# Re-ordering weight-sum stores, row gathers and the first pair of a conditional block kernel

## The chip, the cores and the metric

The kernel runs on one core of a Trainium2 chip. The metric is the device time of one execution in microseconds (us). All tensors are 32-bit floats. The names of the engines are PE (TensorE), DVE (VectorE), ACT (ScalarE), POOL (GpSimd) and SP (SyncE, which here only issues DMAs). ACT and POOL issue DMAs too.

## The reference

An input x of 32 sequences of 128 tokens with 512 features goes through two residual halves. Each half is modulated by a condition vector of the sequence. The first half changes only the tokens that the mask marks (the last few of each sequence, some 500 of 4096); the second changes all tokens.

```python
emb = silu(t) @ ada_w + ada_b
shift, scale, gate_msa = split(emb, 3, axis=1)
norm = _layernorm(x) * (1.0 + scale[:, None]) + shift[:, None]
norm = where(m, norm, 0.0)
fwd = gelu(norm @ ssm_w1 + ssm_b1) @ ssm_w2 + ssm_b2
bwd = flip(... the same with bwd_w1, bwd_b1, bwd_w2, bwd_b2 on flipped tokens ...)
x = x + gate_msa[:, None] * where(m, fwd + bwd, 0.0)
shift_mlp, scale_mlp, gate_mlp = split(silu(t) @ ffada_w + ffada_b, 3, axis=1)
ff_norm = _layernorm(x) * (1.0 + scale_mlp[:, None]) + shift_mlp[:, None]
h = gelu(ff_norm @ ff_w1 + ff_b1)          # 512 -> 1024
return x + gate_mlp[:, None] * (h @ ff_w2 + ff_b2)   # 1024 -> 512
```

## The kernel before

**First half, on slots.** The marked tokens are numbered, and 512 slots of 128-token tiles (slot tiles 0 to 3) take their rows of x by indirect DMA. Slots go in two groups of two tiles: `hidden` computes the first matmul and gelu (`ph_s`, `h_s`), `project` the second matmul (`po_s`), and `keep_slots` the end: bias (L208), gate (L210), adding the slot's x (L301), and a store of the tile to `x1_rows` in DRAM (L302). If there are more than 512 marked tokens a loop at the end of the program takes the rest.

**Second half, in pairs.** The 4096 tokens go in four pairs; a pair p is two sides of four sequences (2 x 512 tokens). For each sequence of a pair, `take_first_half` (L671 to L682) issues one indirect gather on POOL that puts the finished slot rows of `x1_rows` over the rows of x that are already in SBUF; slots past a bound are skipped. Then come the layer norm's statistics (`Statistics.one`, L707 and L708, and `root`, L712 on DVE and the power L713 on POOL), `normalised` (L719), and a turn of tokens into features. The turn is done by DVE's 32 x 32 transpose (L1149 or L1254) and 16 small DMAs (`turned`, L746); ACT then scales and shifts (`scaled`, L729). Side 1 of pair 0 is turned on PE instead (`transposed`, L735, with DVE's scaling L727).

**Matmuls with fewer multiplications.** Both matmuls of the second half are split in two levels of seven products for eight (in the manner of Strassen and Winograd). For this, sums of weight quarters and of token quarters are needed:

- Four weight sums of ff_w1 (`weight_sums(1)` to `(4)`, L584) are computed once, stored to `t_rows` in DRAM (`store_weight_sums`, L588 and L589, two DMAs a sum, 512 and 384 KB), and read back as `tw` (`load_weights`, L853) once a pair for each sum.
- Sum 1 lies in two x tiles (`spare`) that a later load of x (`load_side`, L331) fills; sum 2 in `t_2`; sum 3 in a group of x tiles; sum 4 in a tile with the tag "s12", which pair 0's token sums take over.
- `TokenBlocks.one(1)` to `one(4)` (L776) are token sums of the outer level: s1, s2, the first half of the second side, and s4. `token_sums` (L836 to L846) are those of the inner level.

The first product (ff_w1) is `FirstProduct`. Its seven outer products j are "streams", run in the order `STREAMS = (1, 2, 5, 6, 3, 7, 4)`. Each stream has seven inner phases P1 to P7, four matmuls of 256 columns each (L907). `window(new, old, fill)` runs one stretch of seven phases: P5 and P1 of the new stream, P3 and P7 of the old, P2 and P6 of the new, P4 of the old. After phase n (0 to 6) it issues what was put in `fill[n]`. `put(w, n, f, ...)` asks for `f` after phase n of the window in which `STREAMS[w]` is new. After a phase, results are combined: ACT copies (L921, L953, L965), DVE additions from PSUM (L932, L937, L942, L951), POOL additions between SBUF tiles (`with_p5` L958, `after` L987, `late_sum` L991), and gelu on ACT (L869). The second product (ff_w2, L1087) is `SecondProduct` with its own fourteen steps, P1U, P5U, P1V, P5V and so on; its first steps are interleaved with the last phases of stream 4.

**What sets the order.** The whole program from the first slot on is under a manual schedule: each engine runs its instructions in the order of the program text, and each queue (SP, ACT, POOL) issues its DMAs in that order. The tile framework only adds waits, for data and for buffers that are used again. So an instruction that waits holds all later ones of its engine.

**The places that the change touches.** Pair 0 begins at L1132: five gathers on POOL, statistics of side 0, the root, three more gathers, `gate_rows`, and the store of sum 4 on POOL (L1141). Then come the second slot group's `hidden`, the turn of side 0 on both DMA queues, and the slot tiles 2 and 3 (L1167 to L1183) with side 1's turns between the matmuls of `project`. L1174 stores sums 1 and 2 on SP, L1175 loads half of pair 1's x. L1187 to L1211 are streams 1 and 2 of pair 0, written out by hand. The fills of the windows are put at L1220 to L1272; the gathers and statistics of the next pair are at L1260 to L1272.

Of the kernel before, what the change touches and what calls it, by code (L numbers as in the profile page):

```python
# [9 lines left out]
F32 = mybir.dt.float32  # L10
# [4 lines left out]
ALU = mybir.AluOpType  # L15
# [7 lines left out]
def kernel(  # L23
# [49 lines left out]
    nc = tc.nc  # L73
# [108 lines left out]
    def hidden(xT, n, w, bcol, func, name, pool, parts=range(HC)):  # L182

        h = []
        for f in parts:
            ph = ps_h.tile([P, 512], F32, tag="h", name=f"ph_{name}_{f}")
            for k in range(KC):
                nc.tensor.matmul(  # L188
                    ph[:, :n], w[:, k, ts(f, P)], xT[:, k, :], start=(k == 0), stop=(k == KC - 1)
                )  # L190
            t = pool.tile([P, n], F32, tag="h", name=f"h_{name}_{f}", bufs=HC + 2)
            nc.scalar.activation(t, ph[:, :n], func, bias=biasT[:, bcol + f : bcol + f + 1])  # L192
            h.append(t)
        return h
# [10 lines left out]
    def gated(po, bias, gate, name, between=lambda: None):  # L205

        t = tp.tile([P, D], F32, tag="t", name=f"t_{name}")
        nc.vector.tensor_tensor(t, po, bias, ALU.add)  # L208
        between()
        nc.vector.tensor_tensor(t, t, gate, ALU.mult)  # L210
        return t
# [84 lines left out]
    def finish_slots(at, h1, gate, between=None):  # L296
        keep_slots(at, project(at % (NC // 2), h1, w2, f"s{at}", between), gate)

    def keep_slots(at, po, gate, between=lambda: None):
        t = gated(po, b2, gate, f"s_{at}", between)  # L300
        nc.vector.tensor_tensor(t, t, xc[at], ALU.add)  # L301
        nc.sync.dma_start(x1_rows[ts(at, P), :], t)  # L302
# [98 lines left out]
    slot_row = ssm.tile([P, NS], F32, name="slot_row")  # L401
# [160 lines left out]
    def in_blocks(t):  # L562
        return t.rearrange("p g (h f) -> p (g h) f", f=2 * P)
# [22 lines left out]
    def store_weight_sums(*which, queue=nc.sync):  # L586
        for j in which:
            queue.dma_start(t_rows[j - 1, :, :4], t_sum[j][0])  # L588
            queue.dma_start(t_rows[j - 1, :, 4:], t_sum[j][1][:, :3])  # L589
# [76 lines left out]
    t = in_blocks(sp.tile([P, G, D], F32, tag="s12", name="tw_4"))  # L666
    t_sum[4] = [t[:, :4], t[:, 4:]]
# [464 lines left out]
    take_first_half(0, x_of[0], range(G + 1))  # L1132
    stats = [Statistics(x_of[0][side], f"0_{side}") for side in range(2)]
# [7 lines left out]
    store_weight_sums(4, queue=nc.gpsimd)  # L1141
# [24 lines left out]

    po_s2 = project(0, h1, w2, "s2")  # L1167
# [22 lines left out]
    now.apart(1)  # L1190
    now.do(1, "P1")
# [3 lines left out]
    of_x[0].one(4)  # L1195
# [16 lines left out]
    for p in range(NP):  # L1212
# [25 lines left out]
        if more_pairs:  # L1238
# [33 lines left out]
            put(6, 4, stats[1].root)  # L1272
# [189 lines left out]
```

## Time and profile before

| | us |
|---|---|
| median of 3 runs | 465.46 |
| lowest and highest | 465.28, 465.61 |
| the profiled execution | 467.79 |
| its span, first to last instruction | 466.0 |

The mean granted clock of TensorE is 0.995. Busy times in the span:

| engine | busy us | share |
|---|---|---|
| PE, matmuls | 451.4 | 97% |
| PE, weight loads | 365.3 | 78% |
| DVE | 330.8 | 71% |
| ACT | 175.4 | 38% |
| POOL | 160.0 | 34% |

DMA moved 70.41 MB. The stages on PE's timeline: slots of the first group to 53 us, the second group 59.1 to 88.4, then four pairs. The first product of pair 0 begins at 88.42, its second product at 135.6; later pairs take about 91.5 us each from one second product to the next (the step P5V starts at 148.87, 240.16 and 331.83).

A matmul of 256 columns has a duration of 379 ns in the list of groups, but matmuls overlap: a run of them starts one every 216 ns. So a busy share of 97% isn't the distance to PE's peak; the spacing of the starts is what to read.

In lines of the timeline the columns are start, duration, engine, line, operation, output<-inputs and shape, number of instructions merged, and in brackets the idle time before, with what ended it.

### The profile page before, as it was taken

How to read it: one execution, taken by the hardware profiler on the slowest of the kernel's cores; microseconds unless marked ns; L12 is line 12 of the kernel's file. 1: busy time of each engine (PE TensorE's matmuls, PEld its weight loads, DVE VectorE, ACT ScalarE, POOL GpSimd, SP SyncE). 2: the span in 40 equal slices, each digit the busy share in tenths (PEclk: the TensorE clock that was granted, in tenths of full speed). 3: DMA queues.
4: the chain of work that ended last, by engine and by line, in shares of the span. 5: the costliest groups of instructions: out<-in, count | busy, mean ns of one | idle time of the engine just before them, and what ended most of it. 6: DMA issues, size and time to landing. Idle time of an engine off the chain costs nothing.

```text
span 466.0 us, 5828 instructions
## 1 busy us (share of the span) xinstructions
PE 451.4 (97%) x2000; PEld 365.3 (78%) x2000; DVE 330.8 (71%) x538; ACT 175.4 (38%) x380; POOL 160.0 (34%) x153
## 2 busy tenths in 40 slices
PE   6899999899999999999999999999999999999995
PEld 2385385477788888888888888888888888888884
DVE  4649768969668759996787399867864995434645
ACT  3121021734364371354553713444546144562000
POOL 6210074038973000389710004897000025660000
PEclk9999999989999999999999999999999999999999
DMA  8999716880406752834086438330973342212022
GB/s 277 386 407 355 302 50 140 265 316 22 165 0 198 102 108 86 291 118 162 1 209 101 98 107 313 98 136 3 235 100 73 127 168 79 80 68 114 0 79 105
DMA packets 82418, 70.41 MB, mean 151 GB/s; under 512 B 63168, under 2 KB 63696, under 8 KB 81362
## 3 DMA queue, kind: packets, MB, share of 16 engines
q1 hardware_dynamic: 67298, 57.03, 40.0%
q0 software_dynamic: 4480, 11.66, 7.4%
q10 hardware_dynamic: 10608, 1.32, 2.0%
q8 instruction: 17, 0.28, 0.3%
q14 instruction: 15, 0.12, 0.1%
HBM read 56.83 MB, written 13.17 MB: 150 GB/s over the span
## 4 chain that ended last, share of the span: by engine, by line
PE 74%; POOL 8%; ACT 5%; issue 5%; DVE 4%; DMA 3%; SPq 0%; POOLq 0%; DVEq 0%
PE a_o L1087 19%; PE e_o L1087 16%; PE a_m L907 14%; PE e_m L907 11%; PE ph_s L188 6%; PE po_s L202 4%; POOL hb L991 2%; ACT hb L869 2%; POOL x L675 2%; DMA x<-in_x_dram 2%; DMA tw<-t_rows 1%; POOL ha L958 1%; DVE xT L727 1%; ACT ha L869 1%; PE part_s L283 1%
## 5 line engine op out<-in xcount | busy, mean ns | idle before, releaser
L958 POOL TENSOR_TENSOR ha<-p_m,ha 128x512 f32<-128x512 f32 x20 | 27.4, 1369 | 152.5 <-ACT ha L965 143.3
L1087 PE MATMUL e_o<-fw,ha 128*128 128x256 f32 x256 | 57.9, 379 | 0.0
L729 ACT ACTIVATE xT<-xT,modT 128x128 f32<-128x128 f32 x112 | 44.2, 480 | 29.4 <-DMA xT<-xn 29.4
L1087 PE MATMUL a_o<-t,hb 128*128 128x256 f32 x240 | 54.1, 379 | 0.0
L1087 PEld LDWEIGHTS e_o<-fw,ha 128*128 128x128 f32 x256 | 48.6, 190 | 6.6
L1087 PEld LDWEIGHTS a_o<-t,hb 128*128 128x128 f32 x240 | 45.6, 190 | 6.2
L675 POOL DMA_INDIRECT x<-x_rows,slot_i x32 | 37.5, 1173 | 26.9 <-DMA x_rows<-t_s 18.6
L869 ACT ACTIVATE hb<-hb,biasT 128x256 f32<-128x256 f32 x64 | 29.0, 501 | 28.1 <-POOL hb L991 19.4
L958 POOL TENSOR_TENSOR hb<-p_m,hb 128x512 f32<-128x512 f32 x20 | 28.3, 1415 | 23.0 <-DVE e_m L951 22.7
L921 ACT COPY p_m<-e_m 128x512 f32<-128x512 f32 x27 | 15.8, 586 | 50.1 <-PE e_m L907 50.1
L1087 PE MATMUL e_o<-fw,s 128*128 128x256 f32 x128 | 29.2, 381 | 0.5 <-DVE s L1041 0.3
L965 ACT COPY ha<-e_m 128x512 f32<-128x512 f32 x32 | 18.5, 579 | 28.5 <-PE e_m L907 26.9
L1087 PE MATMUL a_o<-fw,ha 128*128 128x256 f32 x128 | 28.9, 379 | 0.0
L1087 PE MATMUL a_o<-t,s 128*128 128x256 f32 x128 | 28.9, 379 | 0.0
L202 PE MATMUL po_s<-w,h_s 128*128 128x512 f32 x64 | 28.6, 592 | 0.0
L188 PE MATMUL ph_s<-xT_s,w 128*128 128x256 f32 x128 | 28.6, 382 | 0.0
L1087 PEld LDWEIGHTS e_o<-fw,s 128*128 128x128 f32 x128 | 24.1, 190 | 4.8 <-DVE s L1041 1.7
L188 PEld LDWEIGHTS ph_s<-xT_s,w 128*128 128x128 f32 x128 | 24.0, 190 | 4.7 <-ACT h_s L192 1.5
L1087 PEld LDWEIGHTS a_o<-t,s 128*128 128x128 f32 x128 | 24.3, 190 | 3.3
L1087 PEld LDWEIGHTS a_o<-fw,ha 128*128 128x128 f32 x128 | 24.3, 190 | 3.3
L932 DVE TENSOR_TENSOR e_m<-a_m,ha 128x512 f32<-128x512 f32 x20 | 13.9, 696 | 17.6 <-POOL ha L958 7.4
L869 ACT ACTIVATE ha<-e_m,biasT 128x256 f32<-128x256 f32 x48 | 20.1, 469 | 15.8 <-PE e_m L907 8.9
(207 smaller groups left out, 872.3 us busy)
## 6 DMA issues: line engine op xcount, KB each, us to landing
tw<-t_rows SPq DMA_DIRECT2D x16, 896.0 KB, 5.1
x<-in_x_dram SPq DMA_DIRECT2D x16, 512.0 KB, 6.8
gate<-gate_rows POOLq DMA_DIRECT2D x8, 1024.0 KB, 5.3
out_dram<-x SPq DMA_DIRECT2D x15, 512.0 KB, 3.3
xT<-xn SPq DMA_DIRECT2D x92, 64.0 KB, 2.8
fw<-in_L_cond_ff_w_dram SPq DMA_DIRECT2D x2, 2048.0 KB, 10.4
ada_f<-in_L_cond_ffada_w_dram SPq DMA_DIRECT2D x4, 768.0 KB, 15.4
ada_a<-in_L_cond_ada_w_dram SPq DMA_DIRECT2D x4, 512.0 KB, 7.0
```

The costliest lines, as they stand in the source:

```text
L188: nc.tensor.matmul(ph[:, :n], w[:, k, ts(f, P)], xT[:, k, :], start=(k == 0), stop=(k == KC - 1))
L202: nc.tensor.matmul(po, h[f][:, ts(i, P)], w[:, f, :], start=(f == 0), stop=(f == HC - 1))
L675: nc.gpsimd.indirect_dma_start(out=xs[i // G][i % G // 2][:, i % 2], out_offset=None, in_=x1_rows[:slots, :], in_offset=bass.IndirectOffse ...
L729: nc.scalar.activation(out, src, AF.Identity, bias=shift, scale=scale)
L869: nc.scalar.activation(dst[:, n], src[:, n], AF.Gelu_apprx_tanh, bias=biasT[:, f : f + 1])
L907: nc.tensor.matmul(bank[:, ts(n, QT)], self.w_block(j, product)[:, ts(n, P)], self.x_block(j, product), start=(product in ("P1", "P5") and ...
L921: nc.scalar.copy(p5, e)
L932: nc.vector.tensor_tensor(e, a, p5, add)
L958: nc.gpsimd.tensor_tensor(self.place(RESULT[j], c), self.p5[j], other, ALU.add)
L965: nc.scalar.copy(self.place(RESULT[j], c), src)
L991: nc.gpsimd.tensor_tensor(part, self.place("21", c), part, ALU.add)
L1087: nc.tensor.matmul(part, src[:, k, ts(i, P)], w[product][:, k, :], start=(last and k == 0), stop=True, skip_group_check=True,)
```

## The change

The change moves work and leaves the arithmetic as it is.

- Sum 1 is stored from POOL's queue right after pair 0's first five gathers; before, it was stored from SP after slot tile 3's `project`.
- Sum 4 is stored from SP after that `project`, ahead of sum 2; before, from POOL after the gathers. Each store now sends its second part (384 KB) first. Sum 4 lies in a tile with the tag "s4" and a tile that shares its place with `slot_row`, no longer in "s12". The `h` tiles have 8 buffers instead of 10.
- The end of slot tile 2 is split: bias, then side 1's turn 2, then gate, adding x and the store. The end of slot tile 3 is split too: bias, then one(2) and one(3), gate, and after P2, P5 and P6 of stream 1 the adding of x and the store. one(4) moves from after P6 to ahead of all of pair 0's products.
- Gathers for the next pair: four at the end of the window of stream 5 in pair 0 and of stream 2 in pairs 1 and 2, then one in the window of stream 6, one in that of stream 3, two in that of stream 7. Before, pair 0 had all eight in one place, and pairs 1 and 2 had four, two, one and one. With windows and phases: (2, 6) or (1, 6) four, (3, 4) one, (4, 6) one, (5, 4) two.
- Statistics: side 0's root goes to (5, 4) for all pairs (before (3, 6) for pairs 1 and 2). Side 1's four go to (4, 4), (5, 3), (6, 4), (6, 6) instead of (4, 4), (4, 6), (5, 3), (6, 4), and its root to (6, 6) instead of (6, 4).

```diff
-            t = pool.tile([P, n], F32, tag="h", name=f"h_{name}_{f}", bufs=HC + 2)
+            t = pool.tile([P, n], F32, tag="h", name=f"h_{name}_{f}", bufs=HC)
...
-    slot_row = ssm.tile([P, NS], F32, name="slot_row")
+    slot_row = ssm.tile([P, 6 * P], F32, tag="row", name="slot_row")[:, :NS]
...
     def store_weight_sums(*which, queue=nc.sync):
         for j in which:
+            queue.dma_start(t_rows[j - 1, :, 4:], t_sum[j][1][:, :3])
             queue.dma_start(t_rows[j - 1, :, :4], t_sum[j][0])
-            queue.dma_start(t_rows[j - 1, :, 4:], t_sum[j][1][:, :3])
...
-    t = in_blocks(sp.tile([P, G, D], F32, tag="s12", name="tw_4"))
-    t_sum[4] = [t[:, :4], t[:, 4:]]
+    t_sum[4] = [
+        in_blocks(sp.tile([P, KC // 2, G * S], F32, tag="s4", name="tw_4")),
+        ssm.tile([P, 6 * P], F32, tag="row", name="tw_4_b").rearrange("p (b f) -> p b f", b=3),
+    ]
     weight_sums(4)
...
     take_first_half(0, x_of[0], range(G + 1))
+    store_weight_sums(1, queue=nc.gpsimd)
...
     nc.gpsimd.dma_start(gate_rows, mod2[2 * B : 3 * B, :])
-    store_weight_sums(4, queue=nc.gpsimd)
...
+    def with_bias(at, po):
+        tail[at] = tp.tile([P, D], F32, tag="t", name=f"t_s_{at}")
+        nc.vector.tensor_tensor(tail[at], po, b2, ALU.add)
+
+    def with_gate(at, gate):
+        nc.vector.tensor_tensor(tail[at], tail[at], gate, ALU.mult)
+
+    def with_x(at):
+        nc.vector.tensor_tensor(tail[at], tail[at], xc[at], ALU.add)
+        nc.sync.dma_start(x1_rows[ts(at, P), :], tail[at])
+
     po_s2 = project(0, h1, w2, "s2")
 
     def keep_and_turn():
-        keep_slots(2, po_s2, gs[0])
+        with_bias(2, po_s2)
         turn(2)()
+        with_gate(2, gs[0])
+        with_x(2)
 
     po = project(1, h1, w2, "s3", {0: turn(0), 1: turn(1), 2: keep_and_turn, 4: turn(3)})
-    store_weight_sums(1, 2)
+    store_weight_sums(4, 2)
     x_of[1] = [load_side(1, 0, spare)]
     of_x[0] = TokenBlocks(0, xT)
     of_x[0].one(1)
-
-    def outer_sums():
-        of_x[0].one(2)
-        of_x[0].one(3)
-
-    keep_slots(3, po, gs[1], outer_sums)
+    with_bias(3, po)
+    of_x[0].one(2)
+    of_x[0].one(3)
+    with_gate(3, gs[1])
...
     now.apart(1)
+    of_x[0].one(4)
     now.do(1, "P1")
     now.seed(1)
     now.do(2, "P1")
     now.do(1, "P2", "P5", "P6")
-    of_x[0].one(4)
+    with_x(3)
     now.token_sums(1, 0)
...
-            if p == 0:
-                put(2, 6, take_first_half, 1, x_next, range(2 * G))
-            else:
-                put(1, 6, take_first_half, p + 1, x_next, range(G))
-                put(2, 6, take_first_half, p + 1, x_next, range(G, G + 2))
-                put(3, 4, take_first_half, p + 1, x_next, range(G + 2, G + 3))
-                put(5, 4, take_first_half, p + 1, x_next, range(G + 3, 2 * G))
+            put(2 if p == 0 else 1, 6, take_first_half, p + 1, x_next, range(G))
+            put(3, 4, take_first_half, p + 1, x_next, range(G, G + 1))
+            put(4, 6, take_first_half, p + 1, x_next, range(G + 1, G + 2))
+            put(5, 4, take_first_half, p + 1, x_next, range(G + 2, 2 * G))
             for i, at in enumerate(((3, 1), (3, 3), (3, 4), (3, 6))):
                 put(*at, stats[0].one, i)
-            put(*((3, 6) if p else (5, 4)), stats[0].root)
-            for i, at in enumerate(((4, 4), (4, 6), (5, 3), (6, 4))):
+            put(5, 4, stats[0].root)
+            for i, at in enumerate(((4, 4), (5, 3), (6, 4), (6, 6))):
                 put(*at, stats[1].one, i)
-            put(6, 4, stats[1].root)
+            put(6, 6, stats[1].root)
```

More of the change, by code (lines that the diff above doesn't have):

```diff
@@ L203, in project, with gated @@
         return po
-    def gated(po, bias, gate, name, between=lambda: None):
+    def gated(po, bias, gate, name):
         t = tp.tile([P, D], F32, tag="t", name=f"t_{name}")
         nc.vector.tensor_tensor(t, po, bias, ALU.add)
-        between()
         nc.vector.tensor_tensor(t, t, gate, ALU.mult)
@@ L294, in keep_gate, with finish_slots @@
         return t
[L296 to L300, printed above, removed]
+    def finish_slots(at, h1, gate):
+        t = gated(project(at % (NC // 2), h1, w2, f"s{at}"), b2, gate, f"s_{at}")
         nc.vector.tensor_tensor(t, t, xc[at], ALU.add)
@@ L1165, in turn @@
         return lambda: transposed(1, xn_b, xT[1], k)
+    tail = {}
+    def with_bias(at, po):
[6 more added lines that the diff above has]
+        nc.sync.dma_start(x1_rows[ts(at, P), :], tail[at])
     po_s2 = project(0, h1, w2, "s2")
     def keep_and_turn():
-        keep_slots(2, po_s2, gs[0])
+        with_bias(2, po_s2)
         turn(2)()
+        with_gate(2, gs[0])
+        with_x(2)
     po = project(1, h1, w2, "s3", {0: turn(0), 1: turn(1), 2: keep_and_turn, 4: turn(3)})
-    store_weight_sums(1, 2)
+    store_weight_sums(4, 2)
     x_of[1] = [load_side(1, 0, spare)]
```

## The prediction

> **What bounds the kernel now.** I read the page first: TensorE (PE) is busy 97% of the span, and the chain that ended last is 74% PE. So a change pays only where PE's starts come late. I looked for these in the timeline of PE: four matmuls of 256 columns start 0.864 us after the four before them where nothing holds them (102.57, 103.43, 104.29). What the starts take beyond that I call late time. From the first product matmul (88.42) to the second stream's P2 (100.73) eight groups take 12.31 us instead of 6.91: 5.4 us late. The next 31 groups of pair 0 (to 129.57) take 28.84 instead of 26.78: 2.06 late. The same 31 groups of pair 1 (193.90 to 220.85) are only 0.17 late. Later PE is late in one place a pair, 0.3 us before step P5V (148.87, 240.16, 331.83). So some 7.4 us can be won, all of it in the first pair.
>
> The waits of PE, longest first (us in total, times, longest):
>
> ```profile
> PE e_m L907 <- ACT e_m L953: 1.5, 1, 1.5
> PE e_m L907 <- DVE e_m L951: 1.1, 2, 0.7
> ...
> PE a_m L907 <- DVE t_s L208: 0.3, 1, 0.3
> ```
>
> The first is ScalarE's (ACT's) copy L953. The timeline shows why it comes late: ACT issues transposing DMAs until 83.84, waits for their landing, and scales 16 blocks before the copy.
>
> ```profile
> 83.84 1.28 ACT L1152 ACT_TABLE_LOAD   x1 [10.24 <-DMA xT<-xn]
> ...
> 85.60 6.26 ACT L729 ACTIVATE xT<-xT,modT 128x128 f32<-128x128 f32 x16 [0.27 <-DMA xT<-xn]
> ...
> 91.77 0.57 ACT L953 COPY e_m<-a_m_alone 128x512 f32<-128x512 f32 x1
> ...
> 92.40 1.59 PE L907 MATMUL e_m<-xT,fw 128*128 128x256 f32 x4 [1.52 <-ACT e_m L953]
> ```
>
> In the table of stretches (busy times, then clock, DMA share, GB/s) the DMA engines are full at 76 us, with the fourth weight sum among the small packets, and PE's clock is halved at 94 us, just after PE stood:
>
> ```profile
> 76.00:78.00 2.00, 2.00 (x6) 0.88 (x5) 0.78 (x3) 0.00 (x0) 1.04 (x1) 1.00 0.99 237
> ...
> 94.00:96.00 2.00, 2.00 (x6) 1.56 (x6) 0.00 (x0) 0.86 (x2) 0.00 (x0) 0.50 0.91 322
> ```
>
> In pair 0 eight gathers stand in a row on GpSimd (POOL), 104.24 to 116.3, and its sums L958 and L987 come after them; VectorE's (DVE's) L951 and PE wait for them, 0.6 us late at 120.83. Its last gather and the sum behind it:
>
> ```profile
> 115.31 0.99 POOL L675 DMA_INDIRECT x<-x_rows,slot_i  x1 [0.30 <-issue]
> 116.32 1.28 POOL L958 TENSOR_TENSOR ha<-p_m,ha 128x512 f32<-128x512 f32 x1
> ```
>
> The end of pair 1's first product, the place where the change may cost. DVE has no gap from 228.38 to 238.27, and its last link L942 releases an ACT gelu, then L1041, then PE:
>
> ```profile
> 228.38 0.70 DVE L932 TENSOR_TENSOR e_m<-a_m,ha 128x512 f32<-128x512 f32 x1 [1.35 <-POOL ha L958]
> ...
> 229.65 1.75 POOL L958 TENSOR_TENSOR hb<-p_m,hb 128x512 f32<-128x512 f32 x1
> ...
> 230.18 1.50 DVE L719 TENSOR_SCALAR xn<-x,mv,rstd 128x512 f32<-128x512 f32 x1
> ...
> 231.36 1.23 POOL L713 TENSOR_TENSOR rstd<-ve,half 128x4 f32<-128x4 f32 x1
> ...
> 233.54 0.65 DVE L937 TENSOR_TENSOR hb<-a_m,hb 128x512 f32<-128x512 f32 x1
> ...
> 237.59 0.68 DVE L942 TENSOR_TENSOR hb<-a_m,hb 128x512 f32<-128x512 f32 x1
> ...
> 239.42 1.29 DVE L1041 TENSOR_TENSOR s<-hb 128x512 f32<-128x512 f32 x2 [1.15 <-ACT hb L869]
> 240.16 3.32 PEld L1087 LDWEIGHTS e_o<-fw,s 128*128 128x128 f32 x16 [0.56 <-DVE s L1041]
> ```
>
> **What the Trainium skill says.** "SBUF — State Buffer", section Who interferes with whom: a GpSimd operation and a VectorE operation with two SBUF inputs, or a tensor_scalar in its two-port mode, shut each other out for a whole instruction. The trace agrees: L719 takes 0.51 alone and 1.50 beside L958; L712 takes 0.17 alone and 0.30 (226.72, 135.44, 318.39) ending just when a POOL sum ends. "TensorE: Matmul & The Clock Gate", What's actually happening: a free-running window of 3413 ns with too little work halves the clock. The trace has one such stretch of about that length, 92.9 to 96.3. "DMA: Bandwidth & Descriptors", Queues, rings and completion order: each DMA engine takes a queue's descriptors in ring order. The loads tw, issued at 93.85 and 94.3, landed in that order after 6.7 and 8.6 us.
>
> **The change part by part.**
>
> *Store of sum 1 on POOL between gathers 5 and 6.* Two issues of 0.60 and 0.54 us (the rows of the fourth sum's store at 73.07). POOL stood 1.57 us there before L713 (67.30), and DMA is 0.07 busy from 66 to 70. Gathers 6 to 8 land up to 1 us later; their statistics run from 74.17, 2.7 us after the landing of the sixth. Cost 0; if the cover were gone, 1.1.
>
> *Sum 4 leaves POOL.* 0.9 MB leave the stretch where the 16 transposing DMAs move 1.05 MB at about 130 GB/s. At the 385 GB/s of 86 to 90 us it had taken 2.4 us of the engines. So ACT's table load, scaling and copy come 2.4 us earlier: scaling 83.2 to 89.45, the copy right behind PE's first four matmuls (89.5), and P2 starts without a wait. Half of that, 1.2 us, would still leave one(4) below as the later one.
>
> *First pair reordered.* DVE does the same operations. with_bias(2), turn(2), gate and x take 2.7 us as before; the store of slots 2 is issued near 86.35 instead of 85.24, and on SP sums 4 and 2, half a side of x, and the two tw loads stand behind it. one(4) (1.22) moves ahead of L932, to 92.4 to 93.6; the store of sum 4 has landed by 91.4 (issue 87.2, landing 3.6 to 4.2), so it isn't waited for. P6 of stream 1 ends at 93.3 on an unheld PE, so L932 runs 93.6 to 94.25 instead of 97.05. From there with_x (0.6) stands where one(4) stood: L937 95.5, L951 96.1 to 96.8, PE at 96.85 instead of 100.73. Late time 1.5 instead of 5.4, 3.9 won; PE's idle window is gone and with it the half clock, whose 1.7 us are in the 5.4. Then the bill: stream 5 could start at 99.55, and its tw, landed at 100.5 before, has the queue start 1.1 us later and 0.26 MB less ahead (some 0.8 us): about 100.5. 0.9 lost (0 to 2). with_x(3)'s store is now behind the tw loads and lands near 103 instead of 98, so the four gathers run about 103.2 to 109.3; the sums L958 of stream 6 are wanted by 111.6, so this costs nothing.
>
> *Gathers spread.* Pair 0 has four in a row instead of eight. Its 2.06 late falls to about 0.5: 1.5 won. In pairs 1 and 2 there is nothing to win.
>
> *Gathers and statistics late in streams 5 and 6.* The sixth gather is issued near 217.1 in pair 1's times (POOL's sums before it, 1.25 each, end at 216.95) and lands 2.9 later at 220.0; its statistics stand at 219.05 in DVE's order. Then L712 meets the sum L991 (220.75 to 222.0), and L932, before at 220.64, ends near 222.85; PE wants it at 222.58. 0.3 late (0 to 0.9) in each of three pairs. The last two gathers and the root on POOL (1.05 each with gaps) end at 225.7, L991 was free at 225.62: 0.1.
>
> *Last statistics and root to the end of stream 7* (the position 6, 6). On POOL the root no longer stands ahead of L991 (232.57): 1.2 us earlier, but PE waited for DVE there, not for it. On DVE L707, L708 and L712 (0.6 + 0.2 + 0.2, from 225.78) leave a stretch with a gap (1.35 before 228.38) and enter the gapless one, behind L1041 (230.4). L712 arrives at 231.25, is held by L958 to 231.6; L991, which waits already, goes next to 232.95; L719 is held until then. L937 comes at 235.3 instead of 233.54, P4 of stream 4 on PE 0.4 late, L942 at 239.35 instead of 237.59, the gelu 240.05 to 240.95, L1041, PE at 241.7 instead of 240.16: 1.55 a pair. Without the two holds it is 0.6; with gathers of 1.4 instead of 1.05 it is 2.1. Behind L942 stand ACT's gelu and DVE's L1041, and PE has nothing else: it is all lost.
>
> *Buffers* (h two fewer, slot_row and half of sum 4 in one place, sum 4 no longer in s12): no instruction is added, and all earlier readers have ended by 57 us. 0.
>
> **Sum.** Won 3.9 - 0.9 + 1.5 = 4.5. Lost 3 x (1.55 + 0.3 + 0.05) = 5.7. Net +1.2 us. The profiled execution took 467.79 with a span of 466.0, 2.3 above the median of the runs, 465.46. The parts are differences, so they go onto the median: 466.7.
>
> **Rivals.**
> - *The ends of the pairs are cheap* (faster). The place is the DVE row L719 at 230.18: if it gets the port ahead of L991, or L712 isn't held, and the sixth gather lands before 219.5, a pair loses 0.7, not 1.9. Then -4.5 + 2.1 = -2.4: 463.1. For it: L719 (230.18) did get in ahead of L713, which took 1.23 instead of 1.05. Against: L991 would be waiting first. It decides below 1.5 us a pair.
> - *The first pair gives little.* The tw load or the store behind it lands 2 us later still, as SP's queue is full from 86 to 104 us (0.9 to 1.0 busy). Won 2: +3.7, 469.2. Against: fewer bytes are ahead of tw.
> - *The clock falls at P5V.* A gap of 1.5 to 2 us there halves it for a window of 3.4 us, 1.7 lost, in each of three pairs: 466.7 + 5.1 = 471.8. For it: one window with PE about half busy did that at 92.9. Against: this gap is shorter.
>
> **How the numbers follow.** Forecast 0.45, with its own range 465.8 to 468.2; cheap ends 0.27; little won 0.18; clock 0.10. A measurement of this kernel tells 0.2% (0.93 us) from no change. Faster: most of the second, 0.23. Same: the lower third of the forecast (0.15) and the upper edge of the second (0.04), 0.19. Slower 0.58. The range leaves out the clock case and the edges of the second and third: 462.6 to 470.2.
>
> **What would show it.** Right: the copy L953 near 89.5 and no half clock near 94; stream 5 starting 2.5 to 3.5 us earlier; no eight gathers in a row; L719 held behind L991 and PE about 1.5 us later before each of three P5V. Wrong: P5V no more than 0.7 late (then faster), or the transposing DMAs ending at the old time, which would leave L953 as the last wait.

## The result, and the profile after

The changed kernel took 467.57 us (median of 15 runs), the kernel before 465.75 beside it (15 runs): a ratio of 1.0032, 95% interval 1.0018 to 1.0047. It is slower by 1.8 us, where 1.2 were forecast.

The two profiles say something else. The profiled execution of the changed kernel took 466.66 (span 464.8), that of before 467.79 (span 466.0): by them the change won 1.1 us. So the profile of before lies 2.0 us above its median, and the profile after 0.9 below its own. The table splits the spans at four of PE's starts; the last column is a second profile of the changed kernel, from the experiments (467.07, also 0.7 below the median of its runs).

| stretch, us | before | changed | changed, second |
|---|---|---|---|
| to the first product of pair 0 | 88.42 | 88.00 | 87.52 |
| on to stream 5's first product | 15.01 | 12.44 | 11.88 |
| on to P5V of pair 0 | 45.44 | 45.13 | 46.90 |
| on to P5V of pair 1 | 91.29 | 92.77 | 92.68 |
| on to P5V of pair 2 | 91.67 | 92.58 | 92.55 |
| on to the end | 134.17 | 133.88 | 133.87 |
| span | 466.0 | 464.8 | 465.4 |

The first pair wins, later pairs lose 0.9 to 1.5 each. Which waits stand behind this is in the list of PE's waits of the changed kernel (us in total, times, longest). Lines of the helpers are 2 lower here, so that L1085 was L1087, L1039 was L1041, L951 was L953:

```profile
PE e_o L1085 <- DVE s L1039: 3.5, 3, 1.2
...
PE e_m L905 <- DMA tw<-t_rows: 1.1, 1, 1.1
...
PE e_m L905 <- DVE e_m L930: 0.5, 2, 0.2
```

ACT's copy, 1.5 us and first in the list of before, is gone. In its place P5V leads, three times 1.2. The timeline of the changed kernel shows the first pair:

```profile
81.50 1.28 ACT L1150 ACT_TABLE_LOAD   x1 [8.33 <-DMA xT<-xn]
...
83.26 6.26 ACT L727 ACTIVATE xT<-xT,modT 128x128 f32<-128x128 f32 x16 [0.27 <-DMA xT<-xn]
...
89.43 0.57 ACT L951 COPY e_m<-a_m_alone 128x512 f32<-128x512 f32 x1
...
90.10 1.09 PE L905 MATMUL e_m<-xT,fw 128*128 128x256 f32 x4
...
100.44 1.10 PE L905 MATMUL e_m<-sx,tw 128*128 128x256 f32 x4 [1.09 <-DMA tw<-t_rows]
```

The transposing DMAs released ACT 2.34 us earlier (81.50 instead of 83.84), the scaling starts at 83.26 instead of 85.60, and the copy at 89.43 no longer holds PE: P2 follows at 90.10 with no wait in brackets. At 100.44 PE stands 1.09 for the weight sum tw. In the table of stretches PE's clock, the figure before the DMA share, is whole where it was 0.50 in the profile of before:

```profile
94.00:96.00 2.00, 1.97 (x8) 1.41 (x8) 1.97 (x4) 0.40 (x1) 0.00 (x0) 1.00 0.82 256
```

The end of pair 1's first product in the changed kernel:

```profile
225.51 0.70 DVE L930 TENSOR_TENSOR e_m<-a_m,ha 128x512 f32<-128x512 f32 x1 [1.69 <-POOL ha L956]
...
226.79 1.74 POOL L956 TENSOR_TENSOR hb<-p_m,hb 128x512 f32<-128x512 f32 x1
...
227.32 0.69 DVE L705 BATCH_NORM_STATS2 st<-x 128x6 f32<-128x512 f32 x1
...
228.04 0.18 DVE L706 BATCH_NORM_AGGREGATE mv<-st 128x2 f32<-128x6 f32 x1
...
228.25 0.31 DVE L710 TENSOR_SCALAR ve<-mv 128x4 f32<-128x4 f32 x1
...
228.47 1.57 DVE L717 TENSOR_SCALAR xn<-x,mv,rstd 128x512 f32<-128x512 f32 x1
228.50 1.26 POOL L989 TENSOR_TENSOR hb<-hb 128x512 f32<-128x512 f32 x1
...
235.94 0.68 DVE L940 TENSOR_TENSOR hb<-a_m,hb 128x512 f32<-128x512 f32 x1
...
237.59 1.29 DVE L1039 TENSOR_TENSOR s<-hb 128x512 f32<-128x512 f32 x2 [0.97 <-ACT hb L867]
```

DVE has no gap from 225.51 to 236.62. From L930 to L940 it takes 10.43 us; the same stretch of before (L932 at 228.38 to L942 at 237.59) took 9.21. L710 ends within 0.03 us of POOL's L956 (228.56 and 228.53), and L717, which takes 0.50 to 0.53 in its next three places, takes 1.57 beside POOL's L989 (228.50 to 229.76).

### The profile page after: what moved, and what is told of

It is laid out like the page before. It is cut to its first block, busy times and chain, and to the rows that moved or that the text cites. A ratio compares the mean times of both kernels' runs of the same rounds, so it can differ in the third digit from the quotient of the medians.

```text
span 464.8 us, 5830 instructions
## 1 busy us (share of the span) xinstructions
PE 447.9 (96%) x2000; PEld 364.2 (78%) x2000; DVE 333.4 (72%) x538; ACT 176.2 (38%) x380; POOL 158.5 (34%) x153
## 3 DMA queue, kind: packets, MB, share of 16 engines
q10 hardware_dynamic: 10608, 1.32, 2.0%
## 4 chain that ended last, share of the span: by engine, by line
PE 57%; DVE 9%; POOL 4%; DMA 4%; issue 3%; ACT 2%; POOLq 0%; SPq 0%; ACTq 0%
PE a_o L1085 19%; PE e_o L1085 16%; PE a_m L905 12%; PE e_m L905 10%; DMA x<-x_rows,slot_i 2%; DVE xn L717 2%; DMA tw<-t_rows 2%; POOL ha L956 1%; DVE hb L940 1%; POOL hb L985 1%; ACT hb L867 1%; DVE xn L1267 1%; POOL ha L989 1%; DVE st L705 1%; DVE s L1039 1%
## 5 line engine op out<-in xcount | busy, mean ns | idle before, releaser
L956 POOL TENSOR_TENSOR ha<-p_m,ha 128x512 f32<-128x512 f32 x20 | 27.5, 1373 | 158.8 <-ACT ha L963 146.3
L1085 PE MATMUL e_o<-fw,ha 128*128 128x256 f32 x256 | 57.9, 379 | 0.0
L1085 PE MATMUL a_o<-t,hb 128*128 128x256 f32 x240 | 54.1, 379 | 0.0
L1085 PEld LDWEIGHTS e_o<-fw,ha 128*128 128x128 f32 x256 | 48.6, 190 | 6.6
L1085 PEld LDWEIGHTS a_o<-t,hb 128*128 128x128 f32 x240 | 45.6, 190 | 6.2
L673 POOL DMA_INDIRECT x<-x_rows,slot_i x32 | 36.3, 1133 | 30.1 <-DMA x_rows<-t_s 22.7
L956 POOL TENSOR_TENSOR hb<-p_m,hb 128x512 f32<-128x512 f32 x20 | 28.3, 1415 | 19.1 <-DVE hb L935 18.8
L1085 PE MATMUL e_o<-fw,s 128*128 128x256 f32 x128 | 29.2, 381 | 3.5 <-DVE s L1039 3.5
L1085 PEld LDWEIGHTS e_o<-fw,s 128*128 128x128 f32 x128 | 24.1, 190 | 7.8 <-DVE s L1039 4.7
L1085 PE MATMUL a_o<-t,s 128*128 128x256 f32 x128 | 28.9, 379 | 0.0
L1085 PE MATMUL a_o<-fw,ha 128*128 128x256 f32 x128 | 28.9, 379 | 0.0
L705 DVE BATCH_NORM_STATS2 st<-x 128x6 f32<-128x512 f32 x32 | 21.8, 683 | 7.6 <-DMA x<-x_rows,slot_i 7.6
L1085 PEld LDWEIGHTS a_o<-t,s 128*128 128x128 f32 x128 | 24.3, 190 | 3.3
L1085 PEld LDWEIGHTS a_o<-fw,ha 128*128 128x128 f32 x128 | 24.3, 190 | 3.3
```

The source lines that it names most:

```text
L673: nc.gpsimd.indirect_dma_start(out=xs[i // G][i % G // 2][:, i % 2], out_offset=None, in_=x1_rows[:slots, :], in_offset=bass.IndirectOffse ...
L705: nc.vector.bn_stats(st, self.tile_at(i))
L956: nc.gpsimd.tensor_tensor(self.place(RESULT[j], c), self.p5[j], other, ALU.add)
L1085: nc.tensor.matmul(part, src[:, k, ts(i, P)], w[product][:, k, :], start=(last and k == 0), stop=True, skip_group_check=True,)
```

## The experiments

Times are medians, with the runs of the kernel before on the same chip in brackets and the ratio to them with its 95% interval. "Late" is the time between PE's starts beyond 0.864 us per group, as in the prediction.

### Are the profiles usual executions?

**before_again**, the kernel before with no edit, a yardstick for scatter and half clock.

> The kernel before once more, for its clock in several executions. Theory 1: the stretch of half clock at 92.9 to 96.3 us of the first profile (1.7 us lost) is rare; most executions have a mean clock of 0.998 or more and take about 465.6 us, and in a profile without it the first product of pair 0 starts its stream 5 near 101.7 instead of 103.43. Rival: most executions have it, mean clock about 0.995, and the median of 465.75 contains the 1.7 us.

Measured: 465.99 (466.04), 0.9995 [0.9983, 1.0007]. Its profile again has P2 late by 2.2 us and the half clock behind it.

**after_again**, the changed kernel with no edit.

> The changed kernel unchanged, for its scatter and a second profile. Two readings of the sign of the result. Theory H (the half clock in the profile of before is not of its usual execution): the median is 467.5 again with the granted clock at 0.998 to 1.000 in nearly every execution, and the profile shows P5V 1.33 late three times, stream 7's P3 about 0.4 late, no half clock near pair 0. Rival T (the profile of the changed kernel was one of its luckier executions, because the wait for the weight sums tw varies): in this profile the wait for tw before stream 5's first product is not 1.1 but 1.5 to 3, and the span is over 465.5.

Measured: 467.81 (465.85), 1.004 [1.0024, 1.0055]. Each run comes with its mean granted clock, and that settles H. A window of 3.4 us at half speed lowers the mean over 466 us by 0.5 x 3.4 / 466 = 0.0037, to 0.996 at most. (The clock is halved again after the last matmul, in these profiles for at most 2.3 us of the span, which alone leaves 0.998.) Of 185 executions of the kernel before in this study, 37 have 0.996 or less, and their median is 467.17; the other 148 have 465.75. (Eleven more beside root_alone, left out here, have none.) The profile of before (0.995) is of the kind of the 37. Of 32 executions of the changed kernel one is that low. So executions like that of the profile of before are 1.4 us slower, and about one in five is of this kind. The mean doesn't say where in an execution the half clock stood.

Rival T failed as written: the wait for tw was 0.53 here, shorter than in the first profile. But the second profile shows another place that varies. Its list of waits has L930 at 1.7 where the first had 0.5. Its timeline:

```profile
103.49 1.12 POOL L673 DMA_INDIRECT x<-x_rows,slot_i  x1 [4.14 <-DMA x_rows<-t_s]
...
104.92 2.27 POOL L673 DMA_INDIRECT x<-x_rows,slot_i  x1 [0.30 <-issue]
...
107.49 1.83 POOL L673 DMA_INDIRECT x<-x_rows,slot_i  x1 [0.30 <-ACT p_m L919]
...
124.70 0.69 DVE L705 BATCH_NORM_STATS2 st<-x 128x6 f32<-128x512 f32 x1 [1.81 <-DMA x<-x_rows,slot_i]
...
125.53 1.40 DVE L710 TENSOR_SCALAR ve<-mv 128x4 f32<-128x4 f32 x1
...
126.84 0.69 DVE L930 TENSOR_TENSOR e_m<-a_m,ha 128x512 f32<-128x512 f32 x1
...
127.58 1.13 PE L905 MATMUL e_m<-s,tw 128*128 128x256 f32 x4 [1.17 <-DVE e_m L930]
```

and the same place in the first profile:

```profile
124.99 0.70 DVE L705 BATCH_NORM_STATS2 st<-x 128x6 f32<-128x512 f32 x1 [1.93 <-DMA x<-x_rows,slot_i]
...
125.82 0.35 DVE L710 TENSOR_SCALAR ve<-mv 128x4 f32<-128x4 f32 x1
126.08 0.69 DVE L930 TENSOR_TENSOR e_m<-a_m,ha 128x512 f32<-128x512 f32 x1
```

The second and third gather take 2.27 and 1.83 us on POOL (1.11 and 1.00 in the first profile), and POOL is then later for the whole of pair 0. DVE waits about as long for the sixth gather in both (1.81 and 1.93). The difference is the small L710 behind it: here it comes when POOL's sum L989 begins (125.63 to 126.89) and takes 1.40, in the first profile it comes near that sum's end (124.88 to 126.14) and takes 0.35. L930 follows: stream 7's P3 is 1.34 late instead of 0.41. Stream 3's P3, one window earlier, is 0.51 late instead of not at all; there L930 waits 1.06 us for POOL's later sums.

### Each part alone

**first_pair**: the changed kernel with the fills as before (stores, buffers and the reordered pair 0 kept).

```diff
-            put(2 if p == 0 else 1, 6, take_first_half, p + 1, x_next, range(G))
-            put(3, 4, take_first_half, p + 1, x_next, range(G, G + 1))
-            put(4, 6, take_first_half, p + 1, x_next, range(G + 1, G + 2))
-            put(5, 4, take_first_half, p + 1, x_next, range(G + 2, 2 * G))
+            if p == 0:
+                put(2, 6, take_first_half, 1, x_next, range(2 * G))
...
-            for i, at in enumerate(((4, 4), (5, 3), (6, 4), (6, 6))):
+            for i, at in enumerate(((4, 4), (4, 6), (5, 3), (6, 4))):
...
-            put(6, 6, stats[1].root)
+            put(6, 4, stats[1].root)
```

> Stores, buffers and first pair as changed; gathers and statistics in the streams as before. Eight gathers in a row now wait for the store of slot tile 3, which lands near 104, so they run 104.1 to 116.3 as in the first profile, although PE is 2.6 us earlier. Theory 1 (no half clock in a usual execution of before, there they end at 114.6): 0.5 to 1.5 us slower than before. Rival (half clock usual in before): no change to 0.5 us faster. A plain adding of my sum (3.9 won, 0.9 lost, gathers apart) says 3 us faster.

Measured: 469.27 (466.04), 1.0054 [1.0035, 1.0074]. Slower than either kernel. Sixteen of its 22 runs have a mean clock of 0.996 or less (median 469.7), the other six 466.6, so most of the loss comes with half clocks. Its timeline, from the first of the eight gathers on:

```profile
104.12 1.65 POOL L673 DMA_INDIRECT x<-x_rows,slot_i  x1 [3.57 <-DMA x_rows<-t_s]
...
116.03 1.00 POOL L673 DMA_INDIRECT x<-x_rows,slot_i  x1 [0.30 <-issue]
117.04 1.28 POOL L956 TENSOR_TENSOR ha<-p_m,ha 128x512 f32<-128x512 f32 x1
...
118.36 0.70 DVE L930 TENSOR_TENSOR e_m<-a_m,ha 128x512 f32<-128x512 f32 x1 [5.09 <-POOL ha L956]
...
119.11 1.38 PE L905 MATMUL e_m<-xn_sy,tw 128*128 128x256 f32 x4 [4.22 <-DVE e_m L930]
```

Stream 5 starts 11.42 us after pair 0's first product, 3.6 less than in the profile of before. But the first gather now waits for the landing of the last slot rows, until 104.12. In the old order it waited for no landing: it followed POOL's sums, at 104.24 in the profile of before and at 102.27 in a profile without the half clock (fills_only_six, below):

```profile
104.24 1.13 POOL L675 DMA_INDIRECT x<-x_rows,slot_i  x1 [0.17 <-issue]
...
102.27 1.13 POOL L675 DMA_INDIRECT x<-x_rows,slot_i  x1 [0.16 <-issue]
```

PE has run ahead by 3 us to a row of gathers that ends at 117.03 (116.30 before), and stands 4.22 us; a half clock follows (119.9 to 123.3).

**fills_only**: the kernel before with the fills of the changed kernel, so the reverse of the edit above.

> Gathers and statistics in the streams as changed; stores and first pair as before. Won in pair 0 by four instead of eight gathers in a row: 2.0 us. Lost 1.0 us before each of three P5V and 0.4 to 0.5 before stream 7's P3 in each pair: 4.5 us. Together 2.5 us slower than before. Rival (gathers in a row cost nothing in a usual execution): 4.5 us slower.

Measured: 472.45 (466.04), 1.0128 [1.0092, 1.0163], 6 runs. Five of the 6 have a mean clock of 0.996 or less; the other took 470.57. P5V is 1.33 late three times, 3.1 us more than before. The remaining 3 us lie in pair 0, where I had expected a gain. Its timeline there:

```profile
111.83 1.38 DVE L846 TENSOR_TENSOR xT<-xT,xn_sy 128x512 f32<-128x512 f32 x1
...
112.62 1.71 POOL L958 TENSOR_TENSOR hb<-p_m,hb 128x512 f32<-128x512 f32 x1
...
113.12 1.48 DVE L846 TENSOR_TENSOR s<-s,xn_sy 128x256 f32<-128x256 f32 x1
114.53 0.69 DVE L951 TENSOR_TENSOR e_m<-a_m,ha 128x512 f32<-128x512 f32 x1
...
115.27 1.13 PE L907 MATMUL e_m<-xn_sy,tw 128*128 128x256 f32 x4 [1.91 <-DVE e_m L951]
```

With four gathers POOL is done at 110.0 and puts its sums L958 beside DVE's token sums, which took 0.67 and 0.41 before and take 1.38 and 1.48 here. L951 is 1.4 us later, PE stands 1.91 us, and a second half clock follows (116.5 to 119.9). In the kernel before the eight gathers held POOL's sums back until DVE's stretch was over; in the changed kernel that stretch ends at 109.1 instead of 113.2, ahead of the sums.

**fills_only_six** tests this reading: two more gathers ahead of POOL's sums.

```diff
-            put(2 if p == 0 else 1, 6, take_first_half, p + 1, x_next, range(G))
-            put(3, 4, take_first_half, p + 1, x_next, range(G, G + 1))
-            put(4, 6, take_first_half, p + 1, x_next, range(G + 1, G + 2))
+            if p == 0:
+                put(2, 6, take_first_half, p + 1, x_next, range(G + 2))
+            else:
+                put(1, 6, take_first_half, p + 1, x_next, range(G))
+                put(3, 4, take_first_half, p + 1, x_next, range(G, G + 1))
+                put(4, 6, take_first_half, p + 1, x_next, range(G + 1, G + 2))
```

> The kernel before with the changed fills (472.45), but six gathers instead of four ahead of POOL's two products in pair 0. Theory: the fills alone lost 5 us in pair 0 because POOL, done with four gathers at 110.0, put the product of L958 (1.71 us) beside DVE's L846 (1.38 and 1.48 instead of 0.67 and 0.41), so that L951 was 1.4 us late, PE stood 2.08 and the half clock followed. With six gathers L958 starts behind DVE's gapless stretch: the 2.08 and the half clock near 117 are gone, P5V stays 1.33 late three times; 467.5 to 469.5. Rival: it is the gathers' lateness for the statistics that cost: 472 or more.

Measured: 467.92 (465.85), 1.0045 [1.0028, 1.0062]. The stop at 115 and the half clock behind it are gone, P5V stays 1.33 late: the theory's outcome. This profile also gives what none of before gives, the old first pair without a half clock: P2 is 1.68 late there as well, but the clock stays whole,

```profile
94.00:96.00 2.00, 2.00 (x10) 1.45 (x9) 0.92 (x2) 0.71 (x2) 0.00 (x0) 1.00 0.88 292
```

and stream 5 starts 13.24 us after the first product instead of 15.01.

### What makes P5V late

**last_stats_back**: the last statistics and the root of side 1 back at (6, 4).

```diff
-            for i, at in enumerate(((4, 4), (5, 3), (6, 4), (6, 6))):
+            for i, at in enumerate(((4, 4), (5, 3), (6, 4), (6, 4))):
                 put(*at, stats[1].one, i)
-            put(6, 6, stats[1].root)
+            put(6, 4, stats[1].root)
```

> The changed kernel with side 1's last statistics and its root back at phase 4 of the last window (6, 4) instead of (6, 6). If the three operations on DVE behind L1041 are what makes P5V late, PE's late time before P5V goes from 1.33 back to 0.3 us in three pairs: 3 us faster than the changed kernel, about 464.6, 1.2 us faster than before. Rival (P5V is late because POOL's later sums or ACT's gelu come late with the gathers): at most 1 us faster than the changed kernel. The wait before stream 7's P3 stays in both.

Measured: 465.24 (466.04), 0.9977 [0.9963, 0.9991]. P5V is 0.31 late again in all three pairs, and its wait, first in the list of the changed kernel, is gone from this list, which begins with

```profile
PE e_m L905 <- DVE e_m L930: 0.5, 2, 0.3
```

Against the changed kernel's ratio of 1.0032 to 1.0040 this is 2.5 to 3 us, the whole loss and more.

**stats_back_root_late**: only the statistics go back, the root stays (the first two changed lines of the diff above).

> The changed kernel with the last statistics of side 1 moved from (6,6) back to (6,4) and its root left at (6,6). It takes apart what stands in front of P5V. If the place of the statistics (0.9 us of DVE in the gapless stretch) makes P5V late and the root adds little: P5V 0.4 to 0.6 late, 465.3 to 466.0. If it is the root (L710 and the normalised tile L717 behind it, held by POOL's L989): P5V stays over 1.0 late three times and the time at 467.0 to 467.8.

Measured: 467.69 (465.99), 1.0027 [1.0013, 1.0042]; P5V is 1.33 late three times. So at P5V the place of the statistics is worth nothing, and the root is all. From its timeline in pair 1:

```profile
228.27 1.75 POOL L956 TENSOR_TENSOR hb<-p_m,hb 128x512 f32<-128x512 f32 x1
...
228.80 1.24 DVE L710 TENSOR_SCALAR ve<-mv 128x4 f32<-128x4 f32 x1
...
229.95 1.57 DVE L717 TENSOR_SCALAR xn<-x,mv,rstd 128x512 f32<-128x512 f32 x1
229.97 1.27 POOL L989 TENSOR_TENSOR hb<-hb 128x512 f32<-128x512 f32 x1
```

Without the statistics ahead of it L710, an instruction on 4 numbers a partition, takes 1.24 us instead of 0.31, and it ends at 230.04, with L956 (230.02). The statistics only filled the time in which the root would have been held anyway.

**root_alone**: the reverse, one word of the kernel before.

```diff
-            put(6, 4, stats[1].root)
+            put(6, 6, stats[1].root)
```

> The kernel before with one edit: the root of side 1 at (6,6) instead of (6,4); the statistics, the gathers and the first pair stay. If the root's L712, behind L1041 in DVE's stretch and held there by POOL's L958 until that ends, is the whole of what P5V loses: P5V 1.33 late instead of 0.31 in the three pairs, 3 times 1.02, so 468.6 to 469.4. Rival: in the order of before there is a gap on DVE that takes it, as the last two gathers issue otherwise: P5V under 0.8 late and 466 to 467.5.

Measured: 469.56 (466.38), 1.0072 [1.0049, 1.0096], 6 runs against 11. In the profile P5V is 1.33, 1.33 and 1.32 late: three times 1.02 more, 3.1 us, and its span is 3.2 longer than that of before, with a half clock at the same place in both. The medians differ by 3.2 too, but they aren't alike in clock: five of the 6 runs have a mean of 0.996, none of the 11 beside them is below 0.997, and the one run at full clock took 468.65, 2.3 more. So the 3.1 rests on the profiles; stats_back_root_late and last_stats_back, which differ in the root alone and are alike in clock, differ by 2.4 in their medians. In its timeline both holds stand one behind the other:

```profile
231.50 1.74 POOL L958 TENSOR_TENSOR hb<-p_m,hb 128x512 f32<-128x512 f32 x1
...
232.03 1.24 DVE L712 TENSOR_SCALAR ve<-mv 128x4 f32<-128x4 f32 x1
...
233.19 1.57 DVE L719 TENSOR_SCALAR xn<-x,mv,rstd 128x512 f32<-128x512 f32 x1
233.20 1.26 POOL L991 TENSOR_TENSOR hb<-hb 128x512 f32<-128x512 f32 x1
```

L712 is held to the end of L958. POOL's next sum, L991, starts at 233.20, before L712 has ended (233.27), and L719 behind it takes 1.57 beside L991. In the kernel before L719 stood where L712 stands here, was held by L958 alone, and what POOL did next was the small power L713.

### Can the rest be had?

**late_pairs_as_before**: spread gathers in pair 0 alone, with its last statistics and root at (6, 4); pairs 1 and 2 as in the kernel before.

```diff
+            if p == 0:
+                put(2, 6, take_first_half, p + 1, x_next, range(G))
...
+            else:
+                put(1, 6, take_first_half, p + 1, x_next, range(G))
+                put(2, 6, take_first_half, p + 1, x_next, range(G, G + 2))
+                put(3, 4, take_first_half, p + 1, x_next, range(G + 2, G + 3))
+                put(5, 4, take_first_half, p + 1, x_next, range(G + 3, 2 * G))
...
```

> The changed kernel with the fills of pair 0 kept spread (side 1's last statistics and root at (6,4)), and those of pairs 1 and 2 put back as they were: gathers 4, 2, 1, 1 and the root of side 0 at (3,6). If the late sixth gather behind stream 7's P3 and the late root behind P5V are all that the change costs, P5V is 0.31 late three times, stream 7's P3 is late in pair 0 alone, and the time is 0.5 to 1.0 under the version with the late statistics moved back (465.24): 464.3 to 464.8. Rival: the gathers of pairs 1 and 2 as they were cost something that their spread had saved: 465.2 or more.

Measured: 464.92 (465.85), 0.9972 [0.996, 0.9984]. In the profile the late P3 of stream 7 in pairs 1 and 2 is gone, P5V is 0.31 to 0.33 late, and pair 0 has the long gathers and a P3 1.33 late. Its interval and that of last_stats_back overlap almost wholly, so what the late P3 of the later pairs costs isn't told apart.

**tw_ahead**: the load of the first weight sum ahead of the x loads on SP, on the changed kernel.

```diff
-    x_of[1] = [load_side(1, 0, spare)]
...
-    for j in (1, 2):
-        now.load_weights(j)
+    now.load_weights(1)
+    x_of[1] = [load_side(1, 0, spare)]
+    now.load_weights(2)
```

> The changed kernel with the load of the first weight sum issued on SP ahead of the two x loads for pair 1, instead of behind them. If the wait for tw (1.09 in the profile of the changed kernel) is there in its usual execution, its time falls by 0.8 to 1.5 to about 466.4, and stream 5 of pair 0 starts without a wait for DMA. Rival: the usual execution hardly waits for tw, or DVE's sums set the start anyway: 467.3 to 467.7. A third way: the x rows come late for the first gathers and the first statistics of pair 1 wait: above 468.

Measured: 469.24 (465.85), 1.0062 [1.0044, 1.008], 6 runs. The third way came true. PE's wait for tw is gone, stream 5 starts 11.19 us after the first product, and yet all is later: on SP the load waits for DVE until 92.08 in any case, the x loads now stand behind it, the last slot rows go out at 95.20 instead of 94.53 and the first gather starts at 105.31 instead of 104.12.

**x_rows_first**: on late_pairs_as_before, side 1's x loads on ACT's queue at the place (2, 1).

```diff
-                x_of[1].append(load_side(1, 1))
+                x_of[1].append([x_tile(f"{3 * G + 2 * c}") for c in range(2)])
+                for c in range(2):
+                    b = 3 * G + 2 * c
+                    put(2, 1, nc.scalar.dma_start, x_of[1][1][c], x[b : b + 2].rearrange("b s d -> s b d"))
```

> The version with the fills of pairs 1 and 2 as they were, and the two loads of x for side 1 of pair 1 (1 MB) not on SP straight behind the last store of rows x1, but on ACT's queue about 7 us later, so that 1 MB less runs beside that store. Theory: the first gather starts at 103.5 to 104.2 in every version, whatever PE does before it, because the rows stored at about 94.3 land only then, beside some 4 MB of other transfers. Then the first gather starts 1.5 to 3 us earlier, at 101 to 102.5, the gathers and statistics behind it too, and the time falls by 0.5 to 1.5 from 464.9. Rival: the rows land when what was queued before them has (sums, x and tw), and the later loads do not matter: first gather at 103.5 or later, 464.6 or more.

Measured: 465.00 (465.99), 0.9966 [0.995, 0.9983]. A miss: with 1 MB fewer bytes behind them the rows issued at 94.95 still released the first gather only at 103.66. From issue to gather that is 8.7 us instead of 9.5 (94.37 to 103.91 in late_pairs_as_before), less than the 1.5 to 3 expected, and the time didn't move. The rival's numbers came out; that what is queued ahead of the rows sets their landing was not tested by itself.

**pair0_late_stat**: on late_pairs_as_before, in pair 0 the statistics of the sixth gather at (5, 6), the root of side 0 at (3, 6).

```diff
-            put(*((3, 6) if p else (5, 4)), stats[0].root)
-            for i, at in enumerate(((4, 4), (4, 6), (5, 3), (6, 4)) if p else ((4, 4), (5, 3), (6, 4), (6, 4))):
+            put(3, 6, stats[0].root)
+            for i, at in enumerate(((4, 4), (4, 6), (5, 3), (6, 4)) if p else ((4, 4), (5, 6), (6, 4), (6, 4))):
```

> The version with the fills of pairs 1 and 2 as they were, and in pair 0 the second statistics of side 1 moved from (5,3) to (5,6), the root of side 0 from (5,4) to (3,6). Theory: stream 7's P3 in pair 0 is late because DVE waits for the sixth gather to land (1.84 us) and then holds L710 1.36 us beside POOL, with L930 behind them; moved away, the 1.33 before this product is gone, and the time falls by 0.7 to 1.3 from 464.9 to about 463.9. Rival: L930 is late because of what POOL sends it (ha), which stays: no change, 464.6 to 465.2.

Measured: 465.63 (465.99), 0.9983 [0.9969, 0.9997]; if anything slower than what it started from. The late P3 did go, but the root's power on POOL now stands ahead of POOL's sums:

```profile
115.97 1.04 POOL L711 TENSOR_TENSOR rstd<-ve,half 128x4 f32<-128x4 f32 x1
...
120.74 0.70 DVE L930 TENSOR_TENSOR e_m<-a_m,ha 128x512 f32<-128x512 f32 x1 [2.05 <-POOL ha L985]
```

DVE waits 2.05 us for POOL, and PE is 1.52 late at 121.49 instead of 0.51: the wait has moved one window forward, to P3 of stream 3.

## Why the prediction was right, and where its sum was not

The time, 467.57, lies in the forecast's own range, and the sign was right for the reason given: the end of the pairs loses more than the first pair wins. Two terms were off by more than 1 us, in opposite directions, so that the forecast came close by luck.

- *ACT's copy and the transposing DMAs.* As put: the copy at 89.43 (forecast 89.5), scaling at 83.26 (83.2), no half clock near 94. Which of the moved stores, the buffers and the new order brings it was not tested apart.
- *First pair, 3.9 less 0.9 won.* In the profiles 15.01 fell to 12.44, 2.6 won, near the 3.0. The step that failed is "whose 1.7 us are in the 5.4", taken over to the median. The half clock was there in the profiled execution, but not in 148 of 185. Against the old first pair without it, 13.24 in fills_only_six (one profile), the eight profiles with the new order, tw_ahead left out (11.35 to 12.44, median 11.8), win 1.4, not 3.0. That the profile lay 2.3 us above the median stood in the prediction and was not read as a warning.
- *The wait for tw, 0.9.* 1.09 and 0.53 in the two profiles of the changed kernel: the size was right. Taking it away as tw_ahead did won nothing: the rows that wait on SP behind the load then came later, and the first gather with them.
- *Gathers spread, 1.5 won.* The 2.06 late are gone in the first profile, 0.51 of it is back in the second. But the term isn't a part of its own: first_pair (+3.2 us) and fills_only (+6.4) each lose alone, half clocks included, and together cost 1.8. In the nine profiles with the new order the gathers start with the landing of the slot rows, at 103.4 to 105.3, because their store now stands behind the tw loads. That is 15.2 us or more after the first product, against 14.0 in fills_only_six. The prediction put this later landing at nothing, and with the short row of four gathers it costs nothing that shows; with eight it does (first_pair). So the new order needs the short row, and the short row needs DVE's stretch to end earlier.
- *Sixth gather and P3 of stream 7, 0.3 a pair.* Right in mechanism (DVE waits for the landing, then the root's small instruction is held, then L930) and near in pairs 1 and 2 (0.2 to 0.4). In pair 0 it was 0.41 and 1.34; that the small L710 can meet POOL's sum at its beginning, after long gathers, was not in the sum.
- *P5V, 1.55 a pair.* The two holds came where they were put, L710 by L956, L717 behind L989, and PE is later in three pairs; root_alone shows 1.02 a pair. The step that failed here is the length of the two holds. Counted from the start of L932 (L930 after the change), the prediction ended the first hold at 3.22 us, POOL's L991 at 4.57, and L719 about 0.5 behind that; measured are 3.02, 4.25 and 0.28. Together these make the 0.53 that it had too much. That the statistics cost nothing because they lie inside the first hold was in the prediction, and stats_back_root_late, with the same 1.33, shows it. The 0.1 for the last two gathers went into the sum as 0.05, which changes little.
- *Stores on POOL, buffers: 0.* No wait points at either; neither was tested alone.

In the usual execution the terms as measured are: first pair -1.4, gathers -1.5 to -2.1, P3 of stream 7 +1.1 (first profile) to +1.9 (second), P5V +3.1. That is +0.7 to +2.1, and 1.8 to 2.0 was measured; both profiles of the changed kernel lie below its medians, so its usual losses may be larger than these. The forecast came close since 1.6 too much won in the first pair and 1.6 too much lost at P5V cancelled. The sign needed that too: the prediction saw it turn at 1.5 us lost a pair, and P5V and P3 together lost 1.4 to 1.7. Had the first pair won what was forecast, the time would hardly have moved.

Of the rivals, the cheap ends (0.7 a pair) fell with root_alone, and the halved clock at P5V was in none of the profiles, where PE stands 1.16 us there. "The first pair gives little" came half true: 2.9 to 3.5 won in all, between its 2.0 and the forecast's 4.5. But its reason did not: tw landed as forecast, and the store about 1 us later (first gather at 104.12, forecast 103.2).

The best versions are late_pairs_as_before (464.92) and x_rows_first (465.00), which keep the first pair and the spread of pair 0 and leave the ends of the pairs as they were: 0.3% faster than before and some 2.7 us faster than the change. Why a gather takes 1.1 us in one execution and 2.3 in another at the same place was not settled.

## What to carry to other kernels

Before late time is priced from one profile, set that execution's time and granted clock beside those of many runs: what a half clock shows there may belong to one execution of five. Set medians beside each other only where the clocks are alike, too. An instruction of a few numbers is not cheap by its size: moved into a gapless stretch beside GpSimd's long sums, it took up to the rest of the sum that was running, and the next sum began before the instruction behind it could. And two edits that meet at one wait, here the row of gathers, should be priced together, not added.

## What was not expected of the hardware

- Issuing one of the gathers for pair 1 took GpSimd between 0.99 and 2.48 us; the long ones (1.65 to 2.48) ran beside VectorE's token sums, the ones after that stretch took 1.00. "SBUF — State Buffer" in the Trainium skill, section SBUF: two separate sides, says that a DMA issued from GpSimd has its descriptors written by GpSimd, which VectorE can lock out of the port they share. It says so of VectorE's two-port modes. The token sums are tensor_tensor operations, for which the page's section Who interferes with whom reports no such stall, and the same place also gave 1.11. So the cause of the long gathers is not shown.
- The same section, Who interferes with whom, gives the port to one instruction at a time. The durations agree, and a small instruction waits like a large one: L710, on 4 numbers a partition, took 1.24 (0.17 alone) beside a sum of 1.75, and L717, on 512, took 1.57 (0.51 alone). Who goes first when both sides wait isn't shown. L717 or L719 has its start (228.47, 229.95, 233.19) 0.01 to 0.03 us ahead of the POOL sum that held it, but the instruction before it ends 0.08 to 0.09 us after that start.
- Old first pair, P2 late by 1.59 to 2.22: a half clock followed in the profiles of before, before_again, fills_only and root_alone, and none in that of fills_only_six. The page "TensorE: Matmul & The Clock Gate" in the Trainium skill, section What's actually happening, says that the clock follows the activity in windows of about 3.4 us that run freely, whatever the kernel does. The traces agree: the stretches recorded at full clock are 81.92 us in before, 109.23 in first_pair and 372.05 in root_alone, which are 24, 32 and 109 times 3.413. On this grid one can estimate how long PE is without work in each window, with 0.215 us for a matmul of 256 columns and twice that at half clock. In the 14 profiles, from 85 to 455 us, six windows have 2.1 us or more, and a half clock follows each; all others have 2.0 or less, and none follows. The 2.0 is the window from 89.4 to 92.8 in fills_only_six; fills_only, with P2 even less late (1.59 against 1.68), has 2.1. So the pause in the old first pair lies at the limit, and where the window falls decides. A pause of 1.16 us before P5V stays below it. No run moved the window alone.
